# Second layer, product 1: the first row block over edge lists instead of a dense product

## The chip, the cores and the metric

The kernel runs on one core of a Trainium2 chip. The metric is the time of one execution on the device in microseconds (us). A run gives one time; the median of several runs is compared. The profile is one separate execution, recorded by the hardware profiler.

## The reference

Four graph layers work on the same 4096 x 4096 adjacency matrix `adj` (about 8 non-zero entries a row, symmetric pattern, own entries on the diagonal) and the same 4096 x 128 features `x`. After each, the input is added and rows are normalised. The second layer is the one changed here, a Chebyshev convolution applied twice:

```python
def cheb_conv(x, L, W, b):
    Tx0 = x
    out = Tx0 @ W[0]
    Tx1 = L @ x
    out = out + Tx1 @ W[1]
    for k in range(2, W.shape[0]):          # W.shape[0] is 3
        Tx2 = 2.0 * (L @ Tx1) - Tx0
        out = out + Tx2 @ W[k]
        Tx0, Tx1 = (Tx1, Tx2)
    return out + b
# layer 1, x the normalised output of layer 0
h = elu(cheb_conv(x, adj, W0, b0))          # 128 -> 256
h = elu(cheb_conv(h, adj, W1, b1))          # 256 -> 128
x = layernorm(x + h)
```

So the layer needs products of `adj` with tall matrices. The kernel has four of them: product 1 makes t1 = adj x, product 2 makes t2 = 2 adj t1 - x and from it the hidden features and v; product 3 and product 4 do the same job for the second convolution.

## The kernel before, in words

`adj` transposed lies in memory as 8 x 8 chunks of 1 MB. A chunk (ib, c) holds 512 source rows (block c, four tiles of 128) by 512 target columns (block ib). It is loaded by `chunk` through SP's queue into one of five buffers of the pool `ld`; a buffer is free again when everything that reads it is done, and SP issues loads strictly in order.

`propagate` (L722) runs one product: for each row block ib it goes over the eight chunks c, multiplies each with four 128 x 512 fp32 matmuls (L730; each is two records in the profile) into a bank `pacc`, and after each chunk calls a hook, `seen`. At the end of a block product 1 copies the sum to `t1T` (ACT), transposes it with four TensorE instructions and copies it to `t1` (DVE, L770), and `lists.store(2, ...)` writes the rows to a table in memory.

Because a row of `adj` has few entries, later work runs over edge lists. `lists.take(ib, c, a)` is the search for them: for each of a chunk's four tiles the eight largest entries of every row (MAX8, L1396) and their places (FIND_INDEX8, L1397), both on DVE. On the diagonal (ib == c) ACT first makes a copy, `copied`, in which only the own entry is put to zero. Layer 0 does the search for source block 0 (`first_list`). Product 1 does it for source blocks 1 to 3 in every row block, and for source blocks 4 to 7 (`FAR`) in row blocks 0 and 1 (`LAST`). Product 2 does it for `FAR` in the row blocks 2 to 7.

When block c's searches are complete, `lists.build(c)` makes, in three steps on DVE with a few small matmuls between, six nearest entries a row and up to three extra rows of spilled entries: nine source indices a row. `lists.pairs(c)` then gathers the entries' two values (POOL, 36 indirect DMAs a block, `both_ways`) and `lists.paired(c)` files them. A tile of 128 rows (a unit) of a product over lists is: nine indirect DMAs of rows from a table (`rows_of`, POOL), `lists.weigh` (one ACT scaling, three one-hot tiles, six multiply-adds on DVE) and four 128 x 128 matmuls (the function `product`).

Before the change product 1 is dense in all eight row blocks, in the order 2, 3, 0, 4, 5, 1, 6, 7, and `beside_first` (L758) puts block 0's build and pair gathers beside it. Product 2 leaves out blocks 0 and 1, whose eight units `second_product` (L1593) places by a plan of hooks (one hook a chunk, 48 in all), together with the builds of blocks 1 and 2. Product 3 leaves out blocks 0 to 2.

A scheduler orders the instructions of each engine in this part of the kernel by their dependences and its own estimates. `lists.chained` adds an order of its own: every DVE instruction put through it stays behind the one before. In product 1 before, `take` and `build` are not chained; in product 2 they are, with t2 (`t2_of`, L778) among them:

```python
for ib, blk, p in propagate(lambda jt: t1[:, jt, :], order=[0, 4, 1, 5, 2, 6, 3, 7], seen=second, ...):
    t2T = l1w.tile([P, IB], F32, name="t2T")
    r = t2_of(t2T, p, blk)
    if usual:
        lists.chained(r)
    second_end(ib, t2T)
```

`second_end` needs t2T for its matmuls (L785), then ACT, DVE (`hT`, L720) and more matmuls (L790).

The function for the other path, `network(False)`, runs only when a check fails and takes no part in the profile.

Of the kernel before, what the change touches and what calls it, by code (L numbers as in the profile page):

```python
# [11 lines left out]
F32 = mybir.dt.float32  # L12
# [27 lines left out]
PAIRED = [0, 1, 2]  # L40
LAST = [0, 1]
FAR = [4, 5, 6, 7]
NONE = -1e30


@with_exitstack
def adj_resnorm_d4(ctx: ExitStack, tc: tile.TileContext, x_in, xT_in, adj, adjT, pairs, diag_in, w0g, w0gT, a0, w1a, b1a,
# [94 lines left out]
    def chunk(pool, src, ib, c, name="chunk", pinned=False):  # L142

        t = pool.tile([P, TB, IB], F32, name=name)
        r = nc.sync.dma_start(t, src[ib, c])
        if pinned:
            tc.keep_in_program_order(r)
        return t
# [532 lines left out]
    def network(usual):  # L681

        with ExitStack() as whole:
# [3 lines left out]
            with ExitStack() as first, ExitStack() as l1h_pool:  # L687
# [34 lines left out]
                def propagate(stationary, order=range(NB), beside=None, seen=None, blocks=range(NB)):  # L722


                    for ib in blocks:
                        p = ps_acc.tile([P, IB], F32, name="pacc")
                        for n, c in enumerate(order):
                            a = chunk(ld, adjT, ib, c)
                            for k in range(TB):
                                nc.tensor.matmul(p, stationary(c * TB + k), a[:, k, :], start=n == 0 and k == 0,  # L730
                                                 stop=n == NB - 1 and k == TB - 1)
                            if beside and n == 0:
                                beside(p, ib)
                            if usual and seen:
                                seen(ib, n, c, a)
                        yield ib, slice(ib * IB, (ib + 1) * IB), p
# [14 lines left out]
                def fetch(c, n):  # L751
                    for _ in range(n):
                        next(pairs[c], None)

                made = lists.build(0) if usual else None
                done = []

                def beside_first(ib, n, c, a):  # L758
                    if 0 < c < FAR[0] or ib in LAST and c in FAR:
                        lists.take(ib, c, a)  # L760
                    if (len(done), n) in ((1, 0), (1, 4), (2, 0)):
                        next(made)
                    if len(done) > 2 and n == 3:
                        tc.keep_in_program_order(lists.pause(t1[:, done[-1] * TB, 0:1]))
                        fetch(0, TB * 9 // 4)

                for ib, blk, p in propagate(lambda jt: x[:, jt, :], finished, seen=beside_first, blocks=[2, 3, 0, 4, 5, 1, 6, 7]):
                    nc.scalar.copy(t1T[:, blk], p)
                    q = transpose4(ps_tr, "ptr", lambda k: t1T[:, (ib * TB + k) * P:(ib * TB + k + 1) * P])
                    nc.vector.tensor_copy(t1[:, ib * TB:(ib + 1) * TB, :], q)  # L770
                    done.append(ib)
                    if usual:
                        lists.store(2, ib, t1)

                v = state.tile([P, NT, F], F32, name="v")

# [17 lines left out]
                    if usual:  # L794
                        lists.store(0, ib, v)

                second = second_product(lists, l1w, pairs, t1, t1T, xT, hT, v, done, t2_of, second_end) if usual else None

                for ib, blk, p in propagate(lambda jt: t1[:, jt, :], order=[0, 4, 1, 5, 2, 6, 3, 7], seen=second, blocks=[b for b in range(NB) if not usual or b not in LAST]):
                    t2T = l1w.tile([P, IB], F32, name="t2T")  # L800
# [518 lines left out]
    class Lists:  # L1319
# [3 lines left out]
        def __init__(self, whole, first, layer, own_entries):  # L1323
# [2 lines left out]
            self.psum = first.enter_context(tc.tile_pool(name="ps_u", bufs=2, space=PSUM, reuse_waits="tile"))  # L1326
            dram = enter(name="dram", bufs=1, space=bass.MemoryType.DRAM)
            self.table = dram.tile([N + 1, F + H], F32, name="table")
            self.tables = [dram.tile([N + 1, F], F32, name=f"rows{n}") for n in range(3)]
            self.spread = dram.tile([NB, P, TB * SLOTS], BF16, name="spread")  # L1330
            self.top = state.tile([P, NT, NB, 8], F32, name="top", tag="dv")
            self.at = keep.tile([P, NT - TB, NB, 8], U16, name="at")
# [257 lines left out]
    def tile_of(u):  # L1590
        return PAIRED[u // TB] * TB + u % TB

    def second_product(lists, pool, pairs, t1, t1T, xT, hT, v, done, t2_of, second_end):  # L1593
        units = len(LAST) * TB
        E = NEAR + QT
        late = slice(5 * IB, 8 * IB)
# [7 lines left out]
        def at(h, f, *args):  # L1604
            plan.setdefault(h, []).append(lambda: f(*args))

        def fetch(c, n):
            for _ in range(n):
                next(pairs[c], None)

        def pull(u):
            deque(lists.rows_of(u, got[u], 2), 0)

        def weigh(u):
            here = pool.tile([P, F], F32, name="here2", bufs=1)
            lists.weigh(u, t1[:, tile_of(u), :], got[u], here, got[u][:, E:E + QT, :], True)
            made[u] = here

        def product(u):
            t, k = tile_of(u), u % TB  # L1620
            if k == 0:
                sums[0] = pool.tile([P, IB], F32, name="t2T")
            p = lists.psum.tile([P, P], F32, name="u")
            nc.tensor.matmul(p, made.pop(u), ident, start=True, stop=False)
            for j in range(QT):
                nc.tensor.matmul(p, got[u][:, j, :], got[u][:, E + j, :], start=False, stop=j == QT - 1)
            t2_of(sums[0][:, k * P:(k + 1) * P], p, slice(t * P, (t + 1) * P))
            if k == TB - 1:
                second_end(PAIRED[u // TB], sums.pop(0))
# [5 lines left out]
        at(0, pull, 0)  # L1635
        at(0, pull, 1)
        at(7, fetch, 1, TB * E)
        at(8, lists.paired, 0)
        at(26, lists.paired, 1)
        for u, h in enumerate((9, 11, 27, 30, 33, 35, 41, 44)):  # L1640
            at(h, weigh, u)
# [515 lines left out]
```

## Time and profile before

| | |
|---|---|
| median of 3 runs | 1839.98 us (1831.49 to 1844.66) |
| profiled execution, its own time | 1653.07 us |
| its span, first to last instruction | 1651.2 us |
| mean granted TensorE clock in it | 0.950 |
| TensorE (PE) busy | 1478.5 us, 90% |
| VectorE (DVE) busy | 1138.4 us, 69% |
| GpSimd (POOL) busy | 833.1 us, 50% |
| ScalarE (ACT) busy | 385.5 us, 23% |
| matmuls of product 1, L730 `pacc<-chunk,x` | 512 records, 222.6 us |
| chunk loads | 326 of 1 MB, median 5.4 us from issue to landing |

Layer 0 takes the span up to about 338 us, product 1 reaches to 562, product 2 to about 801. In the views shown below, a line of an engine's instructions in order of time has its start, its duration, engine, line, operation, output and inputs, the number of instructions merged, and in brackets the idle time before and what ended it. A line of waits has who waited, for whom, the total in us, how often, and the longest. The DVE instructions of a chained `build` stand at L1317, a helper's line.

### The profile page before, as it was taken

The page shows a single profiled execution, that of the slowest core. Times are in us where ns is not written, and L with a number is a line of the kernel's source. Part 1 is how long each engine was busy: PE and PEld are TensorE (multiplying, and loading weights), DVE is VectorE, ACT ScalarE, POOL GpSimd, SP SyncE. Part 2 cuts the span into 40 slices and gives each one's busy share as a digit, 9 for nine tenths or more (in the row PEclk, how much of TensorE's full clock was granted, in tenths as well). Part 3 has the DMA queues.
Part 4 walks back from the last instruction along what each step waited for, and adds up shares of the span by engine and source line. Part 5 has one row for each costly group of instructions (what it writes and reads, how often), then busy time and mean ns, then how long its engine had stood idle before and what let it go on. Part 6 is the DMA issues. An engine that isn't in the chain of part 4 may idle for free.

```text
span 1651.2 us, 16460 instructions
## 1 busy us (share of the span) xinstructions
PE 1478.5 (90%) x4744; PEld 714.2 (43%) x4744; DVE 1138.4 (69%) x3203; ACT 385.5 (23%) x693; POOL 833.1 (50%) x1322
## 2 busy tenths in 40 slices
PE   6899999999999999999999999889927689788886
PEld 3344444544444444454444454444413344444444
DVE  5987655789887897988699950455336756556766
ACT  5776540010000011121200000222223111122234
POOL 0000000000242188848486888888648888888841
PEclk9999999999999999999999999999967798889988
DMA  9867776588888885867587888778665677678673
GB/s 374 342 256 301 246 271 233 179 277 299 316 315 320 309 285 195 281 210 274 177 296 248 291 278 305 252 265 287 241 151 153 189 259 244 219 239 278 218 192 95
DMA packets 106972, 419.30 MB, mean 254 GB/s; under 512 B 21556, under 2 KB 44088, under 8 KB 67064
## 3 DMA queue, kind: packets, MB, share of 16 engines
q1 hardware_dynamic: 59984, 360.01, 61.1%
q0 software_dynamic: 22656, 36.17, 8.6%
q10 hardware_dynamic: 24232, 21.98, 4.5%
q8 instruction: 39, 0.64, 0.2%
q14 instruction: 61, 0.50, 0.1%
HBM read 404.39 MB, written 13.70 MB: 253 GB/s over the span
## 4 chain that ended last, share of the span: by engine, by line
PE 46%; DVE 25%; POOL 14%; issue 6%; DMA 6%; ACT 3%; ACTq 0%; DVEq 0%; POOLq 0%
PE pacc L730 15%; PE pacc L423 12%; POOL got L1820 6%; PE pp L2050 5%; DMA got<-table,source 4%; PE pp L1931 3%; POOL got L1518 3%; DVE at L1397 3%; DVE top L1396 2%; POOL idle L1563 2%; DVE here L1556 1%; POOL value L1518 1%; DVE same L1317 1%; DVE gw L1856 1%; DVE acc L1944 1%
## 5 line engine op out<-in xcount | busy, mean ns | idle before, releaser
L1820 POOL DMA_INDIRECT got<-table,source x288 | 275.8, 958 | 88.8 <-issue 62.0
L1931 PE MATMUL pp<-chunk,xT 128*128 128x512 f32 x496 | 244.0, 633 | 1.4 <-ACT xT L1902 0.7
L730 PE MATMUL pacc<-chunk,x 128*128 128x512 f32 x512 | 222.6, 593 | 0.0
L1518 POOL DMA_INDIRECT got<-rows,source x180 | 182.8, 1016 | 67.6 <-issue 38.6
L423 PE MATMUL pacc<-chunk,hw 128*128 128x512 f32 x408 | 188.7, 607 | 0.8 <-DVE hw L466 0.7
L1358 POOL IOTA i<- 128x384 int32 (+3 forms) x4 | 1.0, 238 | 345.7 <-PE pden L411 329.8
L2050 PE MATMUL pp<-chunk,w 128*128 128x512 f32 x384 | 173.1, 600 | 0.0
L730 PE MATMUL pacc<-chunk,t 128*128 128x512 f32 x384 | 171.5, 597 | 0.0
L730 PEld LDWEIGHTS pacc<-chunk,x 128*128 128x128 f32 x512 | 96.0, 190 | 114.7 <-issue 114.6
L730 PE MATMUL pacc<-chunk,v 128*128 128x512 f32 x320 | 144.5, 597 | 0.0
L1396 DVE MAX8 top<-chunk 128x8 f32<-128x512 f32 x196 | 128.5, 677 | 14.1 <-DMA chunk<-in_adjT 14.1
L1931 PEld LDWEIGHTS pp<-chunk,xT 128*128 128x128 f32 x496 | 94.2, 203 | 91.2 <-issue 84.1
L1397 DVE FIND_INDEX8 at<-top,chunk 128x8 uint16<-128x512 f32 x196 | 133.1, 684 | 0.0
L1518 POOL DMA_INDIRECT both_ways<-in_pairs,both_at x108 | 106.6, 987 | 17.4 <-issue 17.1
L423 PEld LDWEIGHTS pacc<-chunk,hw 128*128 128x128 f32 x408 | 75.0, 192 | 92.1 <-issue 86.3
L1563 POOL TENSOR_TENSOR idle<-idle 128x1 f32<-128x1 f32 x489 | 110.3, 226 | 8.6
L730 PEld LDWEIGHTS pacc<-chunk,t 128*128 128x128 f32 x384 | 71.7, 192 | 81.8 <-issue 81.8
L2050 PEld LDWEIGHTS pp<-chunk,w 128*128 128x128 f32 x384 | 71.7, 194 | 78.5 <-issue 77.7
L395 ACT ACTIVATE junk<-chunk 128x2048 fp8e4<-128x2048 f32 x51 | 97.4, 1910 | 29.8 <-DMA chunk<-in_adjT 29.3
L329 DVE TENSOR_SCALAR pos<-chunk 128x2048 bf16<-128x2048 f32 x66 | 80.1, 1219 | 33.7 <-DMA chunk<-in_adjT 32.1
L1863 PE MATMUL u<-gw,into 128*128 128x132 f32 x192 | 33.2, 317 | 68.3 <-DVE gw L1856 68.3
L1556 DVE SCALAR_TENSOR_TENSOR here<-got,back,here 128x128 f32<-128x128 f32 x120 | 42.2, 352 | 67.0 <-DMA got<-rows,source 63.8
(424 smaller groups left out, 2058.7 us busy)
## 6 DMA issues: line engine op xcount, KB each, us to landing
chunk<-in_adjT SPq DMA_DIRECT2D x326, 1024.0 KB, 5.4
keep<-in_adjT SPq DMA_DIRECT2D x13, 1024.0 KB, 11.0
spread<-spread ACTq DMA_DIRECT2D x16, 384.0 KB, 4.5
got<-table,source POOLq DMA_INDIRECT x288
chunk<-in_adjT ACTq DMA_DIRECT2D x4, 1024.0 KB
got<-rows,source POOLq DMA_INDIRECT x180
table<-rows ACTq DMA_DIRECT2D x8, 264.0 KB, 5.2
xT<-in_xT ACTq DMA_DIRECT2D x8, 256.0 KB, 6.5
```

The costliest lines, as they stand in the source:

```text
L329: r = nc.vector.tensor_scalar(pos, a, 0.0, None, op0=ALU.is_gt)
L395: nc.scalar.activation(junk, a, AF.Relu, scale=-1.0, accum_out=bad[:, n:n + 1], saturate=False)
L423: in_order(nc.tensor.matmul(p, hw[:, j * TB + k, :], a[:, k, :], start=first and k == 0, stop=last and k == TB - 1))
L730: nc.tensor.matmul(p, stationary(c * TB + k), a[:, k, :], start=n == 0 and k == 0, stop=n == NB - 1 and k == TB - 1)
L1396: pin(nc.vector.max(self.top[:, t, ib, :], row))
L1397: pin(nc.vector.max_index(self.at[:, t - TB, ib, :], self.top[:, t, ib, :], row))
L1518: tc.keep_in_program_order(nc.gpsimd.indirect_dma_start(out, None, of, bass.IndirectOffsetOnAxis(ap=index, axis=0)))
L1556: pin(nc.vector.scalar_tensor_tensor(here, got[:, j, 0:F], self.back[:, u, j:j + 1], here, op0=ALU.mult, op1=ALU.add))
L1563: return nc.gpsimd.tensor_tensor(self.idle[:, 0:1], of, self.idle[:, 1:2], ALU.mult)
L1820: nc.gpsimd.indirect_dma_start(got[t][:, j, :], None, table, bass.IndirectOffsetOnAxis(ap=lists.source[:, t, j:j + 1], axis=0))
L1931: nc.tensor.matmul(p, y[:, t0 + k, :], a[:, ib % (TB // n), k, :], start=k == 0, stop=k == n - 1)
L2050: nc.tensor.matmul(p, w[:, c * TB + k, :], a[:, k, :], start=n == 0 and k == 0, stop=n == NB - 1 and k == TB - 1)
```

## The change

Row block 0 is no longer in the dense product 1, whose blocks run in the order 2, 3, 4, 5, 1, 6, 7 (56 hooks). A new function `first_product` plans its four units there: the three steps of block 0's build at hooks 2, 6 and 9; eight stores of x to a new table `rows3` at hook 8; the pair gathers at hooks 10, 14, 18 and 22; the 36 row gathers at hook 24; `paired` at 30; the units' weighings at hooks 32, 36, 39 and 43, each unit's matmuls one hook later. The chunks of block 0 are still needed for the lists: chunks (0, 1) to (0, 3) are loaded for the search alone at hooks 13, 27 and 47 of product 1, chunks (0, 4) to (0, 7) at hooks 15, 22, 38 and 46 of product 2. Chunk (0, 0) is not loaded in either. In product 1 all searches, the build, and the copies to `t1` now go through `lists.chained`. `paired(0)` leaves product 2.

```diff
--- before.py
+++ after.py
@@ -40,6 +40,7 @@
 PAIRED = [0, 1, 2]
 LAST = [0, 1]
 FAR = [4, 5, 6, 7]
+SPARE = 0
 NONE = -1e30
 
 
@@ -752,25 +753,21 @@
                     for _ in range(n):
                         next(pairs[c], None)
 
-                made = lists.build(0) if usual else None
                 done = []
 
-                def beside_first(ib, n, c, a):
-                    if 0 < c < FAR[0] or ib in LAST and c in FAR:
-                        lists.take(ib, c, a)
-                    if (len(done), n) in ((1, 0), (1, 4), (2, 0)):
-                        next(made)
-                    if len(done) > 2 and n == 3:
-                        tc.keep_in_program_order(lists.pause(t1[:, done[-1] * TB, 0:1]))
-                        fetch(0, TB * 9 // 4)
-
-                for ib, blk, p in propagate(lambda jt: x[:, jt, :], finished, seen=beside_first, blocks=[2, 3, 0, 4, 5, 1, 6, 7]):
-                    nc.scalar.copy(t1T[:, blk], p)
+                def first_end(ib):
                     q = transpose4(ps_tr, "ptr", lambda k: t1T[:, (ib * TB + k) * P:(ib * TB + k + 1) * P])
-                    nc.vector.tensor_copy(t1[:, ib * TB:(ib + 1) * TB, :], q)
+                    r = nc.vector.tensor_copy(t1[:, ib * TB:(ib + 1) * TB, :], q)
                     done.append(ib)
                     if usual:
+                        lists.chained(r)
                         lists.store(2, ib, t1)
+
+                beside_first = first_product(lists, l1w, pairs, x, t1T, hT, t1, done, first_end, lambda c: chunk(ld, adjT, SPARE, c)) if usual else None
+
+                for ib, blk, p in propagate(lambda jt: x[:, jt, :], finished, seen=beside_first, blocks=[2, 3, 4, 5, 1, 6, 7] if usual else range(NB)):
+                    nc.scalar.copy(t1T[:, blk], p)
+                    first_end(ib)
 
                 v = state.tile([P, NT, F], F32, name="v")
 
@@ -794,7 +791,7 @@
                     if usual:
                         lists.store(0, ib, v)
 
-                second = second_product(lists, l1w, pairs, t1, t1T, xT, hT, v, done, t2_of, second_end) if usual else None
+                second = second_product(lists, l1w, pairs, t1, t1T, xT, hT, v, done, t2_of, second_end, lambda c: chunk(ld, adjT, SPARE, c)) if usual else None
 
                 for ib, blk, p in propagate(lambda jt: t1[:, jt, :], order=[0, 4, 1, 5, 2, 6, 3, 7], seen=second, blocks=[b for b in range(NB) if not usual or b not in LAST]):
                     t2T = l1w.tile([P, IB], F32, name="t2T")
@@ -1326,7 +1323,7 @@
             self.psum = first.enter_context(tc.tile_pool(name="ps_u", bufs=2, space=PSUM, reuse_waits="tile"))
             dram = enter(name="dram", bufs=1, space=bass.MemoryType.DRAM)
             self.table = dram.tile([N + 1, F + H], F32, name="table")
-            self.tables = [dram.tile([N + 1, F], F32, name=f"rows{n}") for n in range(3)]
+            self.tables = [dram.tile([N + 1, F], F32, name=f"rows{n}") for n in range(4)]
             self.spread = dram.tile([NB, P, TB * SLOTS], BF16, name="spread")
             self.top = state.tile([P, NT, NB, 8], F32, name="top", tag="dv")
             self.at = keep.tile([P, NT - TB, NB, 8], U16, name="at")
@@ -1590,7 +1587,69 @@
     def tile_of(u):
         return PAIRED[u // TB] * TB + u % TB
 
-    def second_product(lists, pool, pairs, t1, t1T, xT, hT, v, done, t2_of, second_end):
+    def first_product(lists, pool, pairs, x, t1T, hT, t1, done, first_end, spare_chunk):
+        E = NEAR + QT
+        wide = (E + QT) * P
+        got = [hT[:, u % 2, u // 2 * wide:(u // 2 + 1) * wide].rearrange("p (j f) -> p j f", f=F) for u in range(TB)]
+        made, plan = {}, {}
+
+        def at(h, f, *args):
+            plan.setdefault(h, []).append(lambda: f(*args))
+
+        def fetch(n):
+            for _ in range(n):
+                next(pairs[SPARE], None)
+
+        def pull(u):
+            deque(lists.rows_of(u, got[u], 3), 0)
+
+        def weigh(u):
+            here = pool.tile([P, F], F32, name="here2", bufs=1)
+            lists.weigh(u, x[:, tile_of(u), :], got[u], here, got[u][:, E:E + QT, :], True)
+            made[u] = here
+
+        def product(u):
+            t = tile_of(u)
+            p = lists.psum.tile([P, P], F32, name="u")
+            nc.tensor.matmul(p, made.pop(u), ident, start=True, stop=False)
+            for j in range(QT):
+                nc.tensor.matmul(p, got[u][:, j, :], got[u][:, E + j, :], start=False, stop=j == QT - 1)
+            nc.scalar.copy(t1T[:, t * P:(t + 1) * P], p)
+            if u == TB - 1:
+                first_end(SPARE)
+
+        def take_spare(c):
+            lists.take(SPARE, c, spare_chunk(c), True)
+
+        build = lists.build(SPARE, True)
+        for h in (2, 6, 9):
+            at(h, next, build)
+        for ib in range(NB):
+            at(8, lists.store, 3, ib, x)
+        for h in (10, 14, 18, 22):
+            at(h, fetch, E)
+        for u in range(TB):
+            at(24, pull, u)
+        at(30, lists.paired, SPARE)
+        for u, h in enumerate((32, 36, 39, 43)):
+            at(h, weigh, u)
+            at(h + 1, product, u)
+        for h, c in ((13, 1), (27, 2), (47, 3)):
+            at(h, take_spare, c)
+        hooks = [0]
+
+        def seen(ib, n, c, a):
+            h = hooks[0]
+            hooks[0] += 1
+            if SPARE < c < FAR[0] or ib in LAST and c in FAR:
+                lists.take(ib, c, a, True)
+            for f in plan.pop(h, ()):
+                f()
+            if h == 55:
+                assert not plan and not made
+        return seen
+
+    def second_product(lists, pool, pairs, t1, t1T, xT, hT, v, done, t2_of, second_end, spare_chunk):
         units = len(LAST) * TB
         E = NEAR + QT
         late = slice(5 * IB, 8 * IB)
@@ -1635,7 +1694,8 @@
         at(0, pull, 0)
         at(0, pull, 1)
         at(7, fetch, 1, TB * E)
-        at(8, lists.paired, 0)
+        for h, c in zip((15, 22, 38, 46), FAR):
+            at(h, lambda c=c: lists.take(SPARE, c, spare_chunk(c), True))
         at(26, lists.paired, 1)
         for u, h in enumerate((9, 11, 27, 30, 33, 35, 41, 44)):
             at(h, weigh, u)
```

## The prediction

> **What bounds the kernel now.** I read the page first (shares, slices), then the busy time by stretch for products 1 and 2 of the second layer, then TensorE's and VectorE's instructions in order of time there, then the waits of the load queue.
>
> ```profile
> PE 1478.5 (90%) x4744; PEld 714.2 (43%) x4744; DVE 1138.4 (69%) x3203; ACT 385.5 (23%) x693; POOL 833.1 (50%) x1322
> ```
>
> TensorE leads, but the share is a mean over stages. By stretch (columns: us, PE, PEld, DVE, ACT, POOL, granted clock, DMA share, GB/s):
>
> ```profile
> 339.00:451.00 112.00, 112.00 (x291) 50.21 (x289) 103.38 (x320) 9.36 (x17) 11.50 (x22) 1.00 0.83 295
> 451.00:563.00 112.00, 112.00 (x275) 50.05 (x275) 93.82 (x247) 4.81 (x9) 32.56 (x58) 1.00 0.88 320
> 563.00:636.00 73.00, 70.30 (x202) 32.74 (x200) 67.38 (x196) 6.35 (x10) 55.27 (x93) 1.00 0.77 260
> 636.00:725.00 89.00, 84.71 (x247) 40.24 (x247) 73.71 (x186) 21.66 (x37) 67.17 (x112) 0.96 0.70 241
> 725.00:801.00 76.00, 75.20 (x233) 37.72 (x232) 54.48 (x132) 14.86 (x26) 50.85 (x84) 1.00 0.68 233
> ```
>
> Product 1 (339 to 563) never leaves TensorE idle, and VectorE works 197.2 of 224 us. In product 2 TensorE idles 7.8 of 238 us; the first 73 us have VectorE at 92%. Two TensorE waits there, and a whole block of product 1:
>
> ```profile
> 535.38 26.77 PE L730 MATMUL pacc<-chunk,x 128*128 128x512 f32 x62
> ...
> 636.82 3.78 PE L785 MATMUL pmm<-t2T,W1A 128*128 128x512 f32 x4 [2.96 <-DVE t2T L778]
> ...
> 681.72 1.98 PE L785 MATMUL pmm<-t2T,W1A 128*128 128x512 f32 x4 [1.89 <-DVE t2T L778]
> ```
>
> So TensorE sets product 1, and in product 2 VectorE is so close behind that TensorE already waits for it. The load queue's waits in product 1 say the same: a chunk's buffer is mostly held by TensorE, at times by the list search.
>
> ```profile
> SPq L145 <- PE pacc L730: 129.8, 46, 5.6
> SPq L145 <- DVE at L1397: 53.8, 15, 5.0
> ```
>
> [...] I take stage times from the period of a block, not from busy time. [...] where MAX8 and FIND_INDEX8 of two rows are interleaved (369.28 to 374.32) a row takes 1.26 us, where they alternate in a fixed order (562.04 to 567.62) 1.39. [...]
>
> **The change part by part.**
>
> TensorE, product 1. Block 0's 64 records go; a block's period is 27.94 us (451.71 to 479.65 in the chain), 0.48 of it the four transposes, which stay: -27.5. Four units come, each four small products; product 2's (742.93 to 743.82) take 0.89: +3.6. Net -23.9 us.
>
> Chunks. Block 0 had 8 loads in product 1. Now 3 (for the lists alone) are there and 4 in product 2, one is gone. Added: eight 256 KB stores of x (2.1 MB) and 36 row gathers of 64 KB (2.4 MB). Product 1 then moves 59 x 1.05 + 4.5 = 66.4 MB in some 200 us, 332 GB/s; the busiest stretch of 28 us had 349. Close, costed at nothing; if the cover fails, at most the difference to 308 GB/s (its mean before), 66.4 MB / 308 = 216 us instead of 200, +16.
>
> VectorE, product 1. Four searches leave (32 to 28): 4 x 5.03 = -20.1. All searches are now chained in program order: 25 ordinary ones at 5.56 instead of 5.03, +13.3. The three diagonal ones (ib == c) can no longer be mixed with others; alone a row takes 2.56 us (691.57 to 694.13), 10.2 instead of some 7.1: +9.3. Four weighings at 2.96 (612.23 to 615.19): +11.8. The paired copies: +0.5. Sum +14.8. Before, product 1's own VectorE work was 197.2 less the 8.7 of product 2's first build that already ran before 563: 188.5. After: 203.3, beside 200 us of TensorE. A tie, at the profile's clock.
>
> Where the work falls matters more. In block 1 VectorE has 6 searches (33.4), one diagonal (10.2), three weighings (8.9), a copy (0.7): 53 us in a block of 27.9. A chunk's buffer (five of them) stays taken until its search ends, so TensorE must stall there; and the copy of block 0's rows now stands in the chain behind TensorE's fourth unit, some 4 us of waiting. With 203 + 4 and the last buffers, product 1 ends near 339 + 213 = 552 instead of 562.7: -10 at the profile's clock, not -23.9.
>
> Waits and queues moved. The 36 pair gathers follow the build, and 36 row gathers come behind them: 72 x 1.35 us (572.91 to 574.25) = 97 us of POOL. They start when VectorE has built the list: its layer-0 tail ends near 346, then come the first build step 7.7 (554.3 to 562.0), block 2's searches 21.3 and the later steps 8 to 12, so near 386. POOL was idle there. The first weighing needs 36 + 9 gathers, 386 + 61 = 447; VectorE comes to it after ten ordinary searches, one diagonal and three copies (55.6 + 10.2 + 2.0), near 454. Covered by 7 us; later units by about as much or more. If it isn't, TensorE waits for the missing microseconds once. ACT gets four scaled copies, four block copies and the stores; at 14 of 224 us busy it costs nothing.
>
> Product 2. Four searches come in, at hooks 15, 22, 38 and 46: 4 x 5.56 = 22.2 on VectorE, less 0.5 for the paired copies. The order of instructions shows hook 15's ahead of the second block's t2T and hook 22's ahead of the third's: exactly the two rows above for which TensorE waits. Those 11.1 us are on the path at the profile's clock. The other two fall after 725, where VectorE idles 21.5 of 76 us: hidden. TensorE's two products for block 2 that need no t2T move forward into product 1, nothing in sum.
>
> Sum for the profiled execution (1653.07 us, span 1651.2): -10 + 11 = +1, bounds -24 (all TensorE's time gained, searches hidden) and +22 (nothing gained, all four searches on the path).
>
> The median of the runs is 1839.98, 187 us above that execution, and the profile does not show why. If it is TensorE's clock: the stages from 339 to 1210 (871 us) stream chunks through it; 871 x (1/c - 1) = 187 gives c = 0.82, an estimate. Other causes (slower transfers) would not relieve VectorE. At 0.82 a block is 33.5 us and product 2 has 238 / 0.82 = 290 us for 217 of VectorE (195.6 in the three stretches + 21.7): the searches are hidden. TensorE's saving is 23.9 / 0.82 = 29. Product 1 has 7 x 34 = 238 us for 207 of VectorE; only block 1's pile remains (53 in 34: 19 behind, of which three waiting buffers cover 3 x 4.2), 6 us. -29 + 6 = -23. I take this as the likeliest, because a lower clock gives the size of the 187 us from the stages that TensorE sets, without anything else.
>
> **The rivals.**
> 1. Forecast: TensorE sets both products in the timed runs: 1840 - 23 = 1817. For: PE never idle in product 1. Against: VectorE at 197 of 224 us.
> 2. The extra 187 us are not TensorE's clock; the two queues tie as in the profile: +1 x 1840/1653, 1841. For: clock 1.00 in the trace.
> 3. Slower: VectorE's chained queue. Block 1's pile reaches product 2, whose first build now stands behind the last block's copy; t2T is late in every block, and all four searches are on the path with nothing gained: +22, 1862. It decides as soon as VectorE reaches the first t2T (596 before) later than TensorE. For: the two waits at 636 and 681. Against: VectorE's 21.5 us free after 725.
> 4. Transfers limit product 1: 216 us instead of 200 plus the moved searches half hidden, -23 + 13: 1830. Against: chunk loads land 5.8 us after issue, with five buffers.
> That the change doesn't do what it says I exclude: the order of instructions shows one row block fewer and the four units.
>
> **How the numbers follow.** Forecast 0.46, rival 2 0.30, rival 3 0.14, rival 4 0.10. A measurement here tells about 1%, 18 us, from no change. Faster by more than that: the forecast, whose own spread (1802 to 1826) leaves a little to "same": 0.45. Same: rivals 2 and 4: 0.40. Slower: rival 3 and the tail of 2: 0.15. The range for 8 in 10 reaches from 1802 (29 + all of block 1's pile hidden, and some of product 2's waits) to 1852 (half of rival 3's price); the forecast's own range is 1802 to 1826.
>
> **What would show it.** Right: about 28 us of L730's x group gone; product 1 ends 8 to 24 us earlier; the load queue waits longer for the search; the wait for t2T after the second block grows from 2.96 towards 8 us in the profile. Wrong: no TensorE stall in block 1 (the pile is harmless, gain nearer 29), or t2T waits that grow by 10 us each (rival 3), or TensorE waiting for chunks with VectorE idle (rival 4).

## The result, and the profile after

| | before | after |
|---|---|---|
| median, same session | 1836.01 us (6 runs, 1826.66 to 1844.66) | 1890.68 us (6 runs, 1880.78 to 1895.84) |
| ratio after/before, 95% interval | | 1.0299 (1.0272 to 1.0326): slower |
| profiled execution, own time | 1653.07 us (the trace shown above) | 1884.86 us |
| product 1, start of the first to start of the last matmul | 225.9 us | 271.4 us |
| product 2 | 235.8 us | 318.5 us |

The change makes the kernel 54.7 us slower; 1817 was forecast. This kernel takes about 1650 us in some sessions and 1808 to 1840 in others, the runs of a session being mostly alike, and the trace of before shown above is of the first kind, which I call quiet, while the result and the trace of after are of the second, which I call late. Every ratio below was taken within one session. Times of products run from the start of the first matmul to the start of the last.

The page of after, its busy shares, the chain that ended last, and the largest group of product 1:

```profile
PE 1497.9 (80%) x4708; PEld 719.0 (38%) x4712; DVE 1168.6 (62%) x3239; ACT 387.2 (21%) x700; POOL 877.1 (47%) x1389
...
PE 34%; DVE 30%; another core or an unknown queue 15%; issue 11%; DMA 4%; ACT 4%; POOL 2%; SPq 0%; ACTq 0%; DVEq 0%; POOLq 0%
...
L731 PE MATMUL pacc<-chunk,x 128*128 128x512 f32 x448 | 206.1, 614 | 17.9 <-DMA chunk<-in_adjT 14.9
```

TensorE fell from 90% to 80% although its work shrank. The 64 records of block 0 are gone (448 instead of 512), but the group's busy time fell by 16.5 us only: a record takes 614 ns on average instead of 593, at a granted clock of 0.90 on average instead of 1.00. A quarter of the chain is "another core or an unknown queue" and "issue": time with no releaser in the record. Part of this difference is the session's: before in a late one (e13 below) has TensorE at 84% and 19% of its chain under these two names. By stretch (columns as before):

```profile
335.00:451.00 116.00, 93.50 (x245) 41.64 (x244) 83.80 (x256) 8.56 (x16) 53.30 (x92) 0.90 0.66 223
451.00:610.00 159.00, 127.40 (x324) 57.80 (x325) 113.75 (x264) 7.95 (x17) 32.80 (x56) 0.90 0.71 259
```

TensorE, never idle in product 1 before (nor in e13), idles 54 of 275 us; VectorE (DVE) idles more than before, and the transfers run at 223 and 259 GB/s instead of 295 and 320. So neither VectorE nor the transfers took TensorE's place. TensorE in order of time, around the end of block 4, the third block:

```profile
425.73 4.03 PE L731 MATMUL pacc<-chunk,x 128*128 128x512 f32 x9
430.50 0.67 PE L731 MATMUL pacc<-chunk,x 128*128 128x512 f32 x1 [0.74 <-issue]
433.30 0.59 PE L731 MATMUL pacc<-chunk,x 128*128 128x512 f32 x1 [2.13 <-issue]
437.08 2.08 PE L731 MATMUL pacc<-chunk,x 128*128 128x512 f32 x2 [3.19 <-DMA chunk<-in_adjT]
468.01 1.12 PE L155 MATMUL ptr<-ident,t1T 128*128 128x128 f32 x4 [28.86 <-issue]
```

The block's last matmul is the one at 433.30; the two at 437.08 already belong to the next block, and behind them stand this block's transposes, which need ACT's copy to t1T. ACT, in order of time:

```profile
401.02 0.58 ACT L769 COPY t1T<-pacc 128x512 f32<-128x512 f32 x1 [9.42 <-PE pacc L731]
...
467.37 0.58 ACT L769 COPY t1T<-pacc 128x512 f32<-128x512 f32 x1 [55.07 <-remote]
```

ACT had nothing else to do; the copy starts 33.5 us after the recorded end of that last matmul. TensorE follows the copy at once (467.95 to 468.01). A semaphore is a counter whose movements the trace records and on which the waits in it end. In the trace of before TensorE's has 842 movements for the 840 instructions that name it, and until 1637 us none comes over 0.04 us after the latest recorded end. In after's it moves at 454.50, 460.93 and 467.35, while TensorE has no matmul running, and the load queue is released at the same moments:

```profile
SPq L146 <- PE pacc L731: 75.8, 20, 6.8
SPq L146 <- DVE at L1394: 61.5, 15, 7.5
SPq L146 <- remote: 50.0, 7, 20.6
```

"remote" is the profile's name for a release whose cause it did not find; here they are completions of TensorE that arrive long after its record says it was done. The trace has the recorded end and the release, up to 33.5 us apart (433.89 to 467.35), and nothing between them: which of the two is the late one it does not show.

The lateness builds up. Matched in order with the recorded ends of this block's chunks, the release of the second chunk comes 2 us late (410.61 after 408.33), the third 7 (418.44 after 411.77), the fourth 15 and the fifth 30 (431.91 and 450.19, taken from the load queue, since the semaphore's own record lacks them), and the last three 31 to 34. TensorE's clock did not start it, for it was 1.00 until 434 (columns as above):

```profile
410.00:434.00 24.00, 19.60 (x45) 7.97 (x43) 20.14 (x45) 0.62 (x1) 20.98 (x37) 1.00 0.60 205
434.00:472.00 38.00, 6.07 (x10) 2.73 (x11) 0.00 (x0) 0.58 (x1) 31.67 (x54) 0.51 0.50 172
```

What runs beside it is GpSimd (POOL), one gather every 1.35 us with a pause instruction behind each, from 389.0 to 488.1, almost without a break:

```profile
454.71 0.98 POOL L1515 DMA_INDIRECT hT<-rows,source  x1 [0.15 <-issue]
455.70 0.21 POOL L1560 TENSOR_TENSOR idle<-idle 128x1 f32<-128x1 f32 x1
456.06 0.98 POOL L1515 DMA_INDIRECT hT<-rows,source  x1 [0.15 <-issue]
```

These are the 72 gathers that the change put into product 1. TensorE is not alone: VectorE, which waits for its own MAX8 between these two instructions, and GpSimd, before a pause, are late by over 1 us as well:

```profile
429.95 0.67 DVE L1393 MAX8 top<-chunk 128x8 f32<-128x512 f32 x1
431.92 0.09 DVE L1394 MATCH_VALUE_LOAD at<-top,chunk 128x8 f32 x1 [1.29 <-issue]
...
450.24 0.19 POOL L1560 TENSOR_TENSOR idle<-idle 128x1 f32<-128x1 f32 x1 [1.48 <-remote]
```

In the quiet traces neither of these two waits exceeds 0.04 us anywhere (0.035 and 0.037 us at most in that of before).

In product 2 the waits for t2T, on which the prediction rested, are not among TensorE's long ones; the longest single one, 23.8 us, again has no named cause:

```profile
PE ptr L787 <- issue: 27.7, 2, 23.8
PE u L1683 <- DVE here L1553: 20.9, 3, 19.4
PE pacc L731 <- DMA chunk<-in_adjT: 18.3, 6, 7.3
```

### The profile page after: what moved, and what is told of

Same layout as the page of the kernel before. It is cut to its first block, busy times and chain, and to the rows that moved or that the text cites. A ratio compares the mean times of both kernels' runs of the same rounds, so it can differ in the third digit from the quotient of the medians.

```text
span 1882.8 us, 16542 instructions
## 1 busy us (share of the span) xinstructions
PE 1497.9 (80%) x4708; PEld 719.0 (38%) x4712; DVE 1168.6 (62%) x3239; ACT 387.2 (21%) x700; POOL 877.1 (47%) x1389
## 4 chain that ended last, share of the span: by engine, by line
PE 34%; DVE 30%; another core or an unknown queue 15%; issue 11%; DMA 4%; ACT 4%; POOL 2%; SPq 0%; ACTq 0%; DVEq 0%; POOLq 0%
PE pacc L424 10%; PE pp L2110 6%; DVE at L1394 6%; PE pp L1991 6%; DVE top L1393 5%; PE pacc L731 4%; DVE here L1553 2%; DMA got<-table,source 2%; DVE acc L2004 1%; DVE gw L1916 1%; DVE spread L1314 1%; PE pden L412 1%; POOL got L1880 1%; DVE same L1314 1%
## 5 line engine op out<-in xcount | busy, mean ns | idle before, releaser
L1991 PE MATMUL pp<-chunk,xT 128*128 128x512 f32 x496 | 258.8, 665 | 8.9 <-issue 5.7
L731 PE MATMUL pacc<-chunk,x 128*128 128x512 f32 x448 | 206.1, 614 | 17.9 <-DMA chunk<-in_adjT 14.9
L731 PE MATMUL pacc<-chunk,t 128*128 128x512 f32 x384 | 182.6, 623 | 21.5 <-DMA chunk<-in_adjT 18.3
L1515 POOL DMA_INDIRECT hT<-rows,source x72 | 71.2, 989 | 147.1 <-DVE top L1393 133.4
L1991 PEld LDWEIGHTS pp<-chunk,xT 128*128 128x128 f32 x496 | 99.2, 214 | 102.8 <-issue 94.9
L1393 DVE MAX8 top<-chunk 128x8 f32<-128x512 f32 x196 | 132.7, 677 | 7.8 <-DMA chunk<-in_adjT 7.8
L731 PEld LDWEIGHTS pacc<-chunk,x 128*128 128x128 f32 x448 | 85.6, 197 | 120.9 <-issue 97.8
L1560 POOL TENSOR_TENSOR idle<-idle 128x1 f32<-128x1 f32 x525 | 117.1, 223 | 10.4 <-remote 1.9
L2004 DVE TENSOR_TENSOR acc<-pp,acc 128x512 f32<-128x512 f32 x96 | 62.7, 683 | 64.9 <-remote 35.2
```

Of the source, the lines that this page charges most:

```text
L1393: pin(nc.vector.max(self.top[:, t, ib, :], row))
L1515: tc.keep_in_program_order(nc.gpsimd.indirect_dma_start(out, None, of, bass.IndirectOffsetOnAxis(ap=index, axis=0)))
L1560: return nc.gpsimd.tensor_tensor(self.idle[:, 0:1], of, self.idle[:, 1:2], ALU.mult)
L1991: nc.tensor.matmul(p, y[:, t0 + k, :], a[:, ib % (TB // n), k, :], start=k == 0, stop=k == n - 1)
L2004: nc.vector.tensor_add(acc3[:, blk], p, acc3[:, blk])
```

## The experiments

Theory A: TensorE's completions reach the engines that wait for them late while GpSimd's stream of gathers (gathers one behind the other without a break) runs, and the added stream puts this into product 1. Rivals: TensorE's clock (theory B, the prediction's), VectorE's chained queue, and, for what remains, the place of the added searches.

**Before, recorded again (e1, e10, e13).** No edit but a comment.

> The kernel before, unchanged, recorded once more: its earlier trace is of an execution of 1653 us, its timed runs are near 1836. Theory A (TensorE's completions reach the other engines late while GpSimd's stream of gathers runs): the new trace is near 1836 and shows TensorE idle gaps of over 3 us that add up to some 190 us more than the 66 us of the earlier trace, each beside gathers, with completions of TensorE over 2 us after its last matmul. Theory B (the prediction's: TensorE's clock): a granted clock near 0.85 in products 1 to 4, blocks of some 33 us instead of 27.9, and no new gaps.

> The kernel before, recorded once more, in the hope of a session in which it takes 1834 us as beside the result on record (in the first sessions it took 1650). Theory A (TensorE's completions reach the others late beside streams of gathers): if it takes 1834, its trace has completions of TensorE 5 to 30 us after its last matmul, in products 2 to 4 and the last layer, and fewer or none in product 1, where its pair gathers come in bursts of 20; products 1 to 4 together are some 120 us longer than the 867 us of the first trace. Theory B (TensorE's clock): no late completions, a lower clock instead. If it takes 1650 it repeats the first trace and tells nothing new.

> The kernel before, recorded again. Theory A: where it takes 1834, its trace has TensorE's completions 5 to 30 us late beside streams of gathers, idle gaps of over 3 us of TensorE that add up to some 130 us more than the 66 of the first trace, and product 1, whose gathers come in bursts of 20, within 15 us of its 226. Where it takes 1650: as the first trace.

e1 took 1648.9 us and e10 1647.3 (ratios to before 0.9991 and 0.9989): quiet, and as the first trace. e13 met a late session: 1834.5 us. Its product 1 and product 2 by stretch:

```profile
335.50:562.00 226.50, 226.50 (x580) 102.22 (x579) 197.74 (x568) 14.22 (x26) 44.39 (x80) 1.00 0.86 307
562.00:874.00 312.00, 250.64 (x682) 119.98 (x681) 197.60 (x518) 43.44 (x74) 172.09 (x288) 0.89 0.55 188
```

Product 1 is as in the quiet trace: TensorE never idle, clock 1.00, 225.9 us. Theory B falls where the prediction used it: product 1 has no clock of 0.82 and no block of 33 us. The time above 1653 lies in product 2 (308.6 us instead of 235.8), product 3 (start to start of the next 240.1 instead of 198.8), product 4 (242.0 instead of 242.8: nothing) and the last layer (445.2 instead of 376.6). Product 1's gathers come in four bursts of nine there (not 20, as I had written), 11 us each; product 2 begins with 80 gathers in one stream, from 572.7 on. TensorE in it:

```profile
621.23 0.77 PE L790 MATMUL ptr<-w2x,hT 128*128 128x128 f32 x2 [16.01 <-remote]
...
632.54 0.37 PE L1624 MATMUL u<-ident,here 128*128 128x128 f32 x1 [1.83 <-issue]
633.95 0.57 PE L1626 MATMUL u<-hT 128*128 128x128 f32 x1 [1.04 <-issue]
635.37 0.60 PE L1626 MATMUL u<-hT 128*128 128x128 f32 x2 [0.85 <-issue]
636.82 0.56 PE L1626 MATMUL u<-hT 128*128 128x128 f32 x1 [0.85 <-issue]
```

A wait of 16 us without a named cause, then a matmul or two every 1.41 to 1.45 us, near the 1.35 us from gather to gather; the same spacing stands in after's trace at 430.50 and 433.30 (two steps). TensorE's gaps of over 3 us add up to 167 us from 300 us on, against 66 in the first trace (101 more, where I had expected 130), and its busy time grows by 56 (1534.7 against 1478.5) while its mean clock falls from 0.950 to 0.908. So before suffers in the same way beside its long streams in product 2, product 3 and the last layer, and product 1, with its short bursts, is spared. Length is not the whole of it: product 4 begins with 108 gathers in one stream (1121.1 to 1280.0, 1.48 us apart on average) and takes no longer.

**After in a quiet session (e5), and without pauses (e6).** e5: no edit but a comment. e6:

```diff
             tc.keep_in_program_order(nc.gpsimd.indirect_dma_start(out, None, of, ...))
-            tc.keep_in_program_order(self.pause())
```

> The kernel after, unchanged, in a session in which the kernel before may take 1650 us, as in the first four runs, instead of 1836. Theory A (the loss on record is TensorE's completions that arrive late beside the added gathers): where before has no late completions, after has none either, products 1 and 2 together take about as long as before's 462 us (the prediction's profile sum of +1, bounds -24 and +22), and the time is 1640 to 1672. Rival (VectorE's chained queue costs it everywhere): 1690 to 1710, with products 1 and 2 long by 40 to 55 us.

> The kernel after without the pause instruction behind each gather, so that gathers come some 1.0 us apart instead of 1.35. Theory A: the denser stream of gathers brings completions of TensorE over 5 us after its last matmul and idle gaps of tens of us beside the gathers, 1750 to 2000, also in a session in which after itself has none. If the pauses are only a delay: GpSimd's work gets shorter by some 190 us in all, nothing else changes, and the time is that of after or up to 30 us less.

e5: 1661.4 us, ratio 1.0079 (1.0050 to 1.0108). Its stream of 72 gathers has the same pace (386.6 to 484.2), and ACT's copy for block 4 comes at 428.78 with the transposes behind it:

```profile
414.42 15.19 PE L731 MATMUL pacc<-chunk,x 128*128 128x512 f32 x35
429.44 0.64 PE L155 MATMUL ptr<-ident,t1T 128*128 128x128 f32 x4
429.92 27.63 PE L731 MATMUL pacc<-chunk,x 128*128 128x512 f32 x64
```

No lateness anywhere; product 1 takes 218.3 us and product 2 252.3, against 225.9 and 235.6 in e1. e6: 1649.6 us, ratio 0.9998 (0.9984 to 1.0012): the denser stream did not bring the lateness about. It was only a little denser, a gather every 1.25 us instead of the 1.0 expected. That half of my expectation fell. A stream alone does not make completions late; in a quiet session even the densest tried does nothing (e6, 1.25 us apart), and without the pauses the time is 11.8 us below e5's.

**All of product 1 unchained (e4).** take, build and weigh lose their `True`, and the copies to t1 leave the chain:

```diff
-                lists.take(ib, c, a, True)
+                lists.take(ib, c, a)
```

> The kernel after with product 1's searches, build, weighings and copies to t1 free of the chained order, as they were before the change. Rival (VectorE's chained queue): the searches mix again at 5.03 us and nothing waits behind the copies; product 1 falls from 271 us to 215 to 235 and the time to about 1835. Theory A: at most the 10 to 15 us of VectorE time come back (1870 to 1890), and the gaps beside the gathers stay.

Quiet: 1669.2 us, ratio 1.0117 (1.0101 to 1.0134), 8 us more than e5; product 1 takes 238.6 us instead of 218.3, with one idle gap of 18.3 us for a chunk, and product 2 243.1 instead of 252.3. The chained order is no cost; it is worth 20 us of product 1 and 11 of both products together. In a quiet session this rival falls; for a late one e14 below decides, which keeps the chained order.

**Slower gathers everywhere (e2 on before; e3, e11, e16 on after).**

```diff
-            tc.keep_in_program_order(self.pause())
+            for _ in range(2):
+                tc.keep_in_program_order(self.pause())
```

> The kernel before with two pause instructions instead of one after each indirect gather, so that a gather comes about every 1.7 us instead of every 1.35. Theory A: GpSimd leaves more room between gathers, the late completions go, and the time falls well below 1836 in spite of some 180 us more GpSimd work (1680 to 1780). If the gathers are only work on GpSimd that must be done in time: nothing gained, 1836 to 1900. Theory B: unchanged or slower.

> The kernel after with two pause instructions instead of one after each indirect gather. Theory A: product 1 (271 us in the trace of after) falls to 210 to 235, product 2 (318) to 240 to 270, and the time falls below 1800. Rival (VectorE's chained queue sets the loss): product 1 and 2 keep their 271 and 318 us or grow, since the gathers come later, 1890 to 1930.

> The kernel after with two pause instructions behind each gather, as in e3 (1723.7 us where before takes 1650). Theory A: in a session in which before takes 1834 and after 1890, the longer pauses let the late completions through, and this kernel takes 1720 to 1780, less than before. If the lateness does not come from the stream of gathers: 1890 + 70 = 1960 or more.

> The kernel of e3 again (two pauses behind every one of these gathers). Where before takes 1650 it took 1724 and 1727. Where before takes 1835 to 1840, theory A: the lateness goes in products 1 to 3 altogether (some 70 us in product 2 and 40 in product 3 of before's third record), the slower gathers cost about as much as they did elsewhere, and the last layer keeps its 65 us of lateness, since its gathers come from another line: 1780 to 1800. Rival (slower gathers help only in product 1, where TensorE depends on no gather): 1840 to 1880.

e2, e3 and e11 met quiet sessions and could not test theory A: 1722.7, 1723.7 and 1726.9 us, ratios 1.0444 (1.0423 to 1.0466), 1.0447 (1.0429 to 1.0464) and 1.0462 (1.0432 to 1.0492). There is nothing late to cure there, and with GpSimd's gathers now about 1.6 to 1.8 us apart the whole takes 73 to 77 us more than before beside it. e16 met a late session, before at 1808.4: 1780.7 us, ratio 0.9842 (0.9789 to 0.9895). In products 1 to 4 no movement of TensorE's semaphore in the records (nine in ten are there) comes over 2 us after the latest matmul end recorded ahead of it (in after's on record up to 28.2, at 467.35): product 1 takes 224.8 us, product 2 257.2, both near the 221.9 and 253.2 of e3. The lateness stays in the last layer, whose gathers come from another line (L1881 in e16) and kept their 1.3 us.

**Only the added gathers slower (e14).** A flag doubles the pause around `fetch` and `pull` of `first_product` and nowhere else:

```diff
+            lists.slow = 1
             for _ in range(n):
                 next(pairs[SPARE], None)
+            lists.slow = 0
...
+            lists.slow = 1
             deque(lists.rows_of(u, got[u], 3), 0)
+            lists.slow = 0
...
-            tc.keep_in_program_order(self.pause())
+            for _ in range(1 + self.slow):
+                tc.keep_in_program_order(self.pause())
```

> The kernel after with two pauses instead of one behind the 72 gathers of block 0 in product 1 alone. Where before takes 1650: the first weighing needs 45 gathers, which come 45 x 0.36 = 16 us later, the prediction's cover of 7 us is gone and some 9 us are lost at most: 1661 to 1671. Where before takes 1834: theory A expects product 1 to fall from 271 us to 220 to 240 and the time from 1890 to 1840 to 1860; a rival in which the lateness has nothing to do with the pace of the gathers expects no change or a loss of 10.

A late session, before at 1839.9: 1842.2 us, ratio 1.0013 (0.9991 to 1.0035). The loss of 3% is gone. The control is e12 below, of the same session with the gathers at their old pace: ratio 1.0223, product 1 271.4 us. GpSimd, then TensorE at the places of after's stall:

```profile
440.58 0.98 POOL L1517 DMA_INDIRECT both_ways<-in_pairs,both_at  x1
441.58 0.48 POOL L1563 TENSOR_TENSOR idle<-idle 128x1 f32<-128x1 f32 x2
442.19 0.98 POOL L1517 DMA_INDIRECT both_ways<-in_pairs,both_at  x1
```

```profile
429.24 0.64 PE L155 MATMUL ptr<-ident,t1T 128*128 128x128 f32 x4
429.71 27.82 PE L731 MATMUL pacc<-chunk,x 128*128 128x512 f32 x64
...
468.39 0.80 PE L1621 MATMUL u<-ident,here 128*128 128x128 f32 x2 [4.38 <-DVE here L1556]
```

A gather every 1.61 us instead of 1.35, and product 1 takes 224.6 us instead of 271.4, with nothing late in it; product 2, whose gathers are as before, takes 321.4 and keeps its lateness. All late traces of the change agree: with one pause (after, e7, e8, e9, e12) product 1 takes 269 to 271 us, with two (e14, e15, e16) 222 to 225. The wait of 4.38 us at the first unit is the price: the rows now come after the weighing is due.

**Where the added searches stand (e7, e8, e9, e12), and both cures together (e15, e17).** e7, repeated as e12:

```diff
-        for h, c in zip((15, 22, 38, 46), FAR):
+        for h, c in zip((31, 36, 40, 46), FAR):
```

e8, in product 1; e9 has both edits; e15, repeated as e17, is e14 with the edit of e7:

```diff
-        for h, c in ((13, 1), (27, 2), (47, 3)):
+        for h, c in ((13, 1), (20, 3), (27, 2)):
```

> The kernel after with block 0's four searches of product 2 at hooks 31, 36, 40 and 46 instead of 15, 22, 38 and 46. In the second trace of after product 2 takes 252.3 us, before 235.6. Theory P (the prediction's step: the searches at hooks 15 and 22 are on the path with 11.1 us, later ones are hidden): product 2 falls to 240 to 243, the time by 9 to 12 us to about 1650. Rival Q (VectorE is behind from product 1's end on and stays so until about hook 40; where the searches stand does not matter): product 2 stays at 249 to 253, the time at 1656 to 1662.

> The kernel after with the search of block 0's third spare chunk at hook 20 of product 1 instead of hook 47. Theory R (at product 1's end VectorE, not TensorE, sets the time: 9.6 us of the first build stand behind it in product 2 where before 11 us of it ran ahead of product 2): 5 us less for VectorE at that place, product 1 and product 2's first block together 4 to 6 us shorter, time 1655 to 1658. Rival (the added searches are hidden in product 1, the first block of product 2 is late for another reason): 0 to -2 us.

> The kernel after with both moves: searches of product 2 at hooks 31, 36, 40 and 46, the third spare chunk of product 1 at hook 20. If both theories P and R hold: 1661 - 11 - 5 = 1645, faster than before's 1649. If neither: 1659 to 1662.

> The kernel of e7 again (block 0's searches of product 2 at hooks 31, 36, 40 and 46). Beside e7 the kernel before took 1834, e7 1875.6, and the two kernels that keep product 1's order near 1882 to 1892. Where before takes 1650 and after 1661: theory P (the two early searches are on the path) 1649 to 1652, product 2 at 240 to 243 instead of 252.3; rival Q (VectorE stays behind wherever they stand) 1657 to 1662. Where before takes 1834: near 1876 again.

> The kernel of e14 (two pauses behind block 0's 72 gathers in product 1 alone) with block 0's searches of product 2 at hooks 31, 36, 40 and 46. Where before takes 1835 to 1840: the two parts add up, 1842 less the 11 of e7 and e12, 1828 to 1834, the first version of the change that is not slower than before. Where before takes 1650: 1661 - 11 + up to 9, 1650 to 1659. If the searches' place mattered only because completions were late: 1840 to 1845 and 1661 to 1670.

> The kernel of e15 again. Where before took 1808 it took 1801.6, 0.990 of before. Where before takes 1650: the searches' better place (theory P, 11 us) against the lost cover of the first weighing (up to 9 us): 1650 to 1659, so 1.000 to 1.006 of before, against 1.008 for after. If theory P does not hold in such a session: 1661 to 1670. Where before takes 1835 to 1840: 0.990 to 0.997 of before.

| | before beside it | this | ratio, 95% interval |
|---|---|---|---|
| e7 | 1834.2 | 1875.6 | 1.0231 (1.0193 to 1.0268) |
| e12 | 1839.9 | 1879.5 | 1.0223 (1.0186 to 1.0261) |
| e8 | 1834.2 | 1891.6 | 1.0319 (1.0278 to 1.0360) |
| e9 | 1834.2 | 1881.7 | 1.0259 (1.0223 to 1.0295) |
| e15 | 1808.4 | 1801.6 | 0.9895 (0.9857 to 0.9932) |
| e17 | 1648.3 | 1659.8 | 1.0058 (1.0041 to 1.0076) |

e7, e8 and e9 were meant for a quiet session and met a late one. Later searches shorten product 2 from 318.5 to 298.6 us in both e7 and e12, though only to 312.5 in e9, and the whole by some 0.7%. The earlier spare search (e8) does nothing that can be told from after, and e9 is no better than e7; in a late session theory R (VectorE sets product 1's end) is neither shown nor refuted by that, because product 1's end is set by the late completions. e17 is quiet: product 2 takes 240.6 us instead of e5's 252.3, the 11 us of theory P (the two early searches are on the path) to within one; product 1 takes 225.8 instead of 218.3, the lost cover, 7.5 us; and product 3 gives back another 8 (204.7 instead of 196.5), which I have not followed up. In a late session the version is a little faster than before: the ratio of e15 rests on 6 of its 20 runs, those below 1795 us, and the medians in the table give 0.996. In a quiet one it is still 0.6% slower. None of those measured in both kinds beats before in both.

## Why the prediction was wrong, point by point

- **The step that failed: "If it is TensorE's clock ... c = 0.82".** The 187 us between before's trace and its runs were read as a lower clock, which would have made TensorE's saving worth 29 us and hidden the searches. e13 shows in their place: clock 1.00 and blocks of 28.0 us (450.2 to 478.2) in product 1, and late completions beside long streams of gathers in product 2, product 3 and the last layer. The profile had been taken under other conditions than the runs, which the gap itself said; a cause that no line showed was given the weight of the likeliest case. Every clock record of before's trace and of after's is 0.5 or 1, and the means are 0.950 and 0.901, not 0.82.
- **Waits and queues moved: "Covered by 7 us".** Right for what it asked: in the quiet e5 the first unit waits for nothing, and in e14, with the rows later, it waits 4.38 us. Wrong in the question: the 72 gathers were priced as work that GpSimd must finish in time, not for what an unbroken stream of 97 us does to others. In the late session that is +45.5 us (271.4 against 225.9), which the sum had at nothing, and nearly all of the loss. e14, which touches nothing but their pace, takes it away.
- **TensorE, -23.9, and product 1 ending near 552 instead of 562.7, -10.** In e5 it ends at 554, 7.6 us shorter than in e1. The size came out near where completions are prompt, the path did not: TensorE was to stall for chunks in block 1, and its waits for chunks in the whole of product 1 are 2.3 us. From copy to copy block 1 takes 28.8 us, and block 6 takes 38.2: TensorE idles 3.0 us there, 2.7 of them for the units' weighings, and works longer, with three of the four units in it.
- **VectorE, "203.3, beside 200 us of TensorE. A tie".** It holds at the end of product 1 in e5, where VectorE works without a break from 539 to past 556.65, past TensorE's end; in the whole of it VectorE is busy for 194.8 of 218.5 us. Chaining was costed at +13.3 and +9.3 and is in truth a gain (e4). The "row" of that sum is a tile of 128 rows. Why it takes 1.39 us in a fixed order (562.04 to 567.62) and 1.26 interleaved (369.28 to 374.32) no run shows.
- **Product 2, "+11" for the two early searches.** The term itself measured 11.7 (e5 to e17). But product 2 grew by 16.7, and its first t2T comes 43.5 us after its start instead of 34.1. In e1 VectorE has finished the first build's first step (to 562.6, first line) before product 1's last copy; in e5 that step stands behind the last copy (the other lines):

```profile
562.43 0.17 DVE L1318 CAST rec<-own 128x4 bf16<-128x4 f32 x1
...
556.65 0.67 DVE L760 COPY t<-ptr 128x512 f32<-128x512 f32 x1
557.24 0.28 DVE L1314 TENSOR_SCALAR there<-top 128x256 f32<-128x256 f32 x1
...
566.84 0.21 DVE L1314 CAST rec<-own 128x4 bf16<-128x4 f32 x1
```

  These 9.8 us are the 8.7 that the prediction took out of product 1 ("less the 8.7 of product 2's first build") and never added to product 2. The term was on record and went missing from the sum. That its absence makes up the rest of the 16.7 is argued from these lines; e8 was to test it and could not. e4 speaks for it: there the step ends at 577.5, before the last copy, the first t2T comes 34.3 us after product 2's start, and product 2 is 9.2 us shorter than in e5. But e4 moves much else too, and 9.2 and 11.7 are more than 16.7 together, so the two must overlap.
- **Where the stalls would show.** A wait for t2T of 8 us was foretold. In e5 the waits for t2T are 2.2 us in all (5.2 in e1), and the load queue has the searches' price instead: it waits 115.7 us for VectorE's search in product 2, against 70.7 in e1, and TensorE waits for chunks:

```profile
PE pacc L731 <- DMA chunk<-in_adjT: 11.1, 3, 5.2
...
PE pmm L782 <- DVE t2T L775: 2.2, 3, 1.0
```

- **Chunks and transfers, costed at nothing.** Right: e5 moves 302 GB/s over product 1, and its only chunk waits there sum to 2.3 us.
- **Sum for the profile, +1, bounds -24 and +22.** Quiet, after is 12.2 us slower in the medians (1661.4 against 1649.2), within the bounds; with the missing 8.7 the sum is +10, and products 1 and 2 of the two traces (-7.6 and +16.7) give +9. Rival 2, the tie, is the right case of a quiet session. Rival 3 named the right sign, but its mechanism is not what the record shows; the loss outside the range has a cause that no rival held.

Open: what makes a session late. It is not the chip alone, for the one that the record calls 1 was quiet for e1 to e4 and late for e12 to e14. Nor is it known whether TensorE's matmuls end late or only their semaphores do, since the traces give one end of a matmul and no second mark of it; its spaced starts beside the gathers (633.95 to 636.82 in e13) suggest that its work is held up too, and not its semaphores alone. One rival is untested, the recording. In the late traces records of semaphores are missing beside gathers, even where nothing is late: in product 1 of e13, 273 of the 576 movements that its gathers make are there, in e1 574. Every timed run comes with a span and a clock of its core, and the profiled execution of after (1884.86 us) is the first of its six timed runs, so no run here is known to be free of recording.

## What to carry to other kernels

When a profile and the timed runs differ by a tenth, as here (1653 against 1840), the profile may be of another condition, as this one was: get a second record of the same kernel before a cause is put on the gap. Price a long run of small indirect gathers not only by when it ends but by its length and pace: in late sessions bursts of nine were harmless here (e13, product 1 at 225.9 us), unbroken streams mostly were not (after, product 1 at 271.4), and 0.26 us more from gather to gather, where there was time for it, removed 47 us (e14, 224.6). When work is taken out of one stage's sum because another stage owns it, write it into that other stage's sum in the same line.

## What the runs showed of the hardware

In a late session TensorE's completions came up to 33.5 us after its recorded ends beside a stream of gathers 1.35 us apart (after, 433.89 to 467.35). The first late one came some 20 us into the stream (410.61 after 389.0 in after), and TensorE then started a matmul or two a gather (e13, 633.95 to 636.82, starts 1.42 to 1.45 us apart). VectorE's and GpSimd's own completions were late beside it too, by 1.29 us (after, 431.92) and by 1.49 us (e13, 633.99). At 1.61 us apart, 72 gathers left product 1 at 224.6 us with nothing late in it (e14), and 108 at 1.48 on average left product 4 at 242.0 us, against 242.8 in the first trace (e13). Fewer movements of semaphores are recorded in the late traces: the trace of a quiet run holds 1480 of one gather semaphore (e5), that of after on record 403, e16's, with slower gathers, 796. In a quiet session gathers without any pause, 1.25 us apart, delayed nothing (e6, 1649.6 us, 0.9998 of before).
